# Two-way attention in exact-split products: the exponentials put in front of the next scaling, and energy's end in another order on VectorE, ScalarE and TensorE

## The chip, the cores and the metric

The kernel runs on one core of one Trainium2 chip. Its time is the device time of one execution in microseconds (us), the median of several runs. A profiled execution beside them gives the trace: every instruction of every engine with its start and its duration. The engines are PE (TensorE, matmuls), PEld (its weight loads), DVE (VectorE), ACT (ScalarE), POOL (GpSimd) and SP (SyncE, which issues DMAs). Each works through its own instructions in the order in which the program was written, and waits where a semaphore says so.

## What is computed

```python
x_q = jnp.einsum('oc,bcn->bno', w_qk, y)
x_k = jnp.einsum('oc,bcn->bon', w_qk, x)
x_v = jnp.einsum('oc,bcn->bon', w_v, x) + b_v[None, :, None]
energy = jnp.einsum('bnc,bcm->bnm', x_q, x_k)
attention = jax.nn.softmax(energy, axis=-1)
attention = attention / (1e-07 + attention.sum(axis=1, keepdims=True))
x_r = jnp.einsum('bcn,bnm->bcm', x_v, attention)
x_r = jax.nn.relu(jnp.einsum('oc,bcn->bon', w_t, x - x_r) + b_t[None, :, None])
return x + x_r
```

x and y (ctx_2048) are 32 x 256 x 1024 in fp32; there are 32 batches b, 256 channels and 1024 columns. The softmax goes along a row of the 1024 x 1024 energy, and the second normalisation along a column.

## The kernel before, in words

Everything stays on the one core, batch by batch (loop at L709). The weights are multiplied together ahead of the loop: energy is y' G x with G = w_qk' w_qk, and the values come with w_t already in them. PSUM's eight banks of 128 x 512 fp32 are one tile, `banks`.

**Energy** (class `Energy`, L420). A batch has NT = 8 tiles of 128 rows. A tile is 128 x 1024 and takes a pair of banks: pair n % 4, that is banks 2(n % 4) and the next, in all batches but the last, which has only three pairs (n % 3). y and G x are each held as three parts (`yf`, `gf`). `first` multiplies two of them, 8 matmuls, and lets ACT multiply the pair by a constant in place (`act.mul`, the "scaling"; for tile 7 each half for itself, right behind its own four matmuls). `second` adds the third part, 4 matmuls, and has DVE take the row's minimum (`nm`, a tensor_reduce over 1024). `exp` is ACT's exponential from the pair into `e`, with the minimum as bias; it sums the row (`rs`). `share` is DVE's reciprocal of that sum (`ri`) and the addition of the scaled row to `acc`, the column sums.

The order is written by hand (L713 to L765): each engine's instructions are issued in the order of the program (class `InOrder`). In iteration n stand first(n), second(n-1), exp(n-2) and share(n-3). On ACT the scaling of tile n so stands in front of the exponential of tile n-2. Below, first(n), scaled(n), second(n), nm(n), exp(n) and share(n) name these pieces of tile n.

**Seven products.** G x, the values and the last product are made by Strassen's scheme in Winograd's form (class `Seven`): seven products P1 to P7 in three banks. A method p1 to p7 is the matmuls of one product; p1, p5 and p6 are followed by ACT's copy out of the bank (`p1s`, `p5s`, `w`), and later products are added onto the same bank: P6, P7 and P4 onto P1's, P3 onto P5's. So P6 needs the copy p1s, P3 needs p5s, and P7 needs w. c11, c12, c22 are DVE's sums of a bank and a copy. For G x (class `Keys`, names with g: gp1s, gp5s, gw, result gfr) the banks are 0, 1, 2; for the values (class `Values`, names with u) 3, 4, 5. Banks 0 to 3 are those of tiles 4 and 5 (L748 on), banks 4 and 5 those of tile 6.

**Energy's end** (L740 to L765). While the last tiles are still at ACT and DVE, PE goes on with the next batch's G x and values. Then come the column sums (`columns`, a DVE instruction, output `parts`), their inverse `rc` on DVE, and the attention product (class `Attention`): DVE normalises the tiles of `e` (`normal`), forms their sums t1 to t4 (`mix`, tile `et`), and PE multiplies them. In the last batch nothing follows; the branch at L766 ends the batch before and then its own attention.

Of the kernel before, what the change touches and what calls it, by code (L numbers as in the profile page):

```python
# [17 lines left out]
def kernel(  # L18
# [26 lines left out]
    NT = N // P  # L45
    MB = 512
    MH = N // MB
# [8 lines left out]
    OVER = 1.0 + 2.0**-12  # L56
# [21 lines left out]
    pe, dve, act, pool = (InOrder(g) for g in (nc.tensor, nc.vector, nc.scalar, nc.gpsimd))  # L78
# [8 lines left out]
    def load(b, pieces=1):  # L87
        to = xp.tile([P, KC, N], F32, tag="x", name=f"x_{b}")
        from_ = x[b].rearrange("(k p) n -> p k n", p=P)
        W = KC // pieces  # L90
        for j in range(pieces):
            nc.sync.dma_start(to[:, ts(j, W)], from_[:, ts(j, W)])
        loaded[b] = to
# [115 lines left out]
    def temp(tag, name):  # L209
        return cp.tile([P, MB], F32, tag=tag, name=name)  # L210
# [8 lines left out]
    def summed(b):  # L219

        s = up.tile([P, 4, MB], F32, tag="xs", name=f"xs_{b}")
        t1, t3, t4, t2 = (s[:, j] for j in range(4))
        to = loaded[b]
        b11, b12 = to[:, 0, ts(0, MB)], to[:, 0, ts(1, MB)]
        b21, b22 = to[:, 1, ts(0, MB)], to[:, 1, ts(1, MB)]
        if b == 0:
            pool.tensor_tensor(t1, b11, b12, ALU.add)
            pool.tensor_tensor(t2, b22, t1, ALU.add)
            pool.tensor_tensor(t3, b12, b22, ALU.add)
            pool.tensor_tensor(t4, b21, t2, ALU.add)  # L230
            steps = []
        else:
            q = quarters(x[b])
            nc.sync.dma_start(s[:, :2], q[:, 0, 1:2, :].to_broadcast([P, 2, MB]))
            nc.sync.dma_start(s[:, 2:], q[:, 1])
            steps = [
                lambda: accumulate(s[:, :2], corners(x[b])),
                lambda: accumulate(s[:, 2:], s[:, 0:1].to_broadcast([P, 2, MB])),
                lambda: accumulate(t4, q[:, 1, 1]),
            ]  # L240
        return (b11, b21, b22, t4, t1, t2, t3), steps
# [178 lines left out]
    class Energy:  # L420
# [21 lines left out]

        def first(self):

            if self.n + 1 < NT:
                self.products((0, 1))
                act.mul(self.pair, self.pair, -OVER)
                return
            for h in range(MH):
                self.products((0, 1), (h,))  # L450
                act.mul(self.pair[:, h], self.pair[:, h], -OVER)

        def second(self):

# [177 lines left out]
    def columns(b):  # L632

        dve.tensor_reduce(
            parts[:, :, 0],
            acc.rearrange("p (j r) -> p j r", r=G32),
            AX.X,
            ALU.add,
            apply_transpose=True,
        )  # L640
# [5 lines left out]
    def inverse(b):  # L646


        sc = one.tile([P, NB, 1], F32, tag="sc", name=f"sc_{b}")
        s = sc[:, :, 0]  # L650
        for a in range(1, NG):
            moved(parts[:G32, :, a], parts[ts(a, G32), :, 0])
        dve.tensor_reduce(s[:G32], parts[:G32], AX.X, ALU.add)
        dve.reciprocal(s[:G32], s[:G32])
        moved(s[G32 : 2 * G32], s[:G32])
        moved(s[2 * G32 :], s[: 2 * G32])
        rc = one.tile([P, NB, G32], F32, tag="rc", name=f"rc_{b}")
        dve.transpose(rc.rearrange("p j r -> p (j r)"), sc.to_broadcast([P, NB, G32]))
        return rc.rearrange("p j r -> p (j r)")
# [8 lines left out]
    g = Keys(0, xr)  # L668
# [40 lines left out]
    for b in range(B):  # L709
        more = b + 1 < B  # L710
        rows = []

        for n in range(NT):  # L713
            now = Energy(b, n, q.to, g.split.to)
            rows.append(now)
            now.first()
            if n == 0:
                e = ep.tile([P, NT, N], F32, tag="e", name=f"e_{b}")
                acc = one.tile([P, N], F32, tag="acc", name=f"acc_{b}")
            if n > 0:  # L720
                rows[n - 1].second()
            if b == 0 and n == 1:
                u.p4()
                u.c21()
                xsteps[1]()
                xsteps[2]()
                ur, usteps = u.factors()
                for step in usteps:
                    step()
            if more and b > 0 and n == 0:  # L730
                load(b + 1)
                xn, xsteps = summed(b + 1)
            if n > 1:
                rows[n - 2].exp()
            if n > 2:
                rows[n - 3].share()
            if more and b > 0 and n in (2, 4, 6):
                xsteps[n // 2 - 1]()

        if more:  # L740
            q = Queries(b + 1)
            for i in range(KC):
                q.load(i, nc.sync.dma_start)
            g = Keys(b + 1, xn)
            rows[-1].second()
            rows[-2].exp()
            rows[-3].share()
            g.p1()  # L748
            rows[-1].exp()
            rows[-2].share()  # L750
            g.p5()
            g.p2()
            g.c11()
            rows[-1].share()
            g.p6()
            columns(b)
            g.p3()
            g.c12()
            g.p7()
            g.c22()  # L760
            un = Values(b + 1, xn)
            un.p1()
            un.p5()
            un.p2()
            un.p6()  # L765
        else:  # L766
            rows[-1].second()
            rows[-2].exp()
            rows[-3].share()
            before.xpart(before.one, 7, True)  # L770
            rows[-1].exp()
            rows[-2].share()
            before.epart(before.one, 7)
            ur, usteps = u.factors()
            now = Attention(b, xr, ur)
            now.begin()
            rows[-1].share()
            columns(b)
            for step in usteps:
                step()  # L780
            before.p7s = temp("w", "p7s")
            act.copy(before.p7s, before.one)
        rc = inverse(b)
        if more:
            q.parts(0)
            q.lower(0)
            un.p3()
            g.p4()
            g.c21()
            un.p7()  # L790
            q.parts(1)
            q.lower(1)
            q.mixed(0)
            g.split.parts(0)
            q.mixed(1)
            g.split.lower(0)

            def between():
                g.split.parts(1)
                g.split.lower(1)  # L800
                g.split.mixed(0)
                g.split.mixed(1)

            now = Attention(b, xr, ur)
            now.begin()
            now.run(un, between=between)
            pool.tensor_copy(behind, now.t4[:, HT - 1, :1])
            if b + 2 < B:
                now.close()
                ur, usteps = un.factors()  # L810
                for step in usteps:
                    step()
            else:
                now.epart(now.two, 3, (3,))
                now.c12()
                now.put()
            before = now
            xr, u = xn, un
        else:
            before.end()  # L820
            now.run(None, before)
            now.finish()
# [30 lines left out]
```

## Time and profile before

| | |
|---|---|
| time, median of 3 runs | 2147.12 us (2146.04 to 2147.6) |
| the profiled execution's own time | 2146.82 us |
| its span, first to last instruction | 2144.9 us |
| mean granted TensorE clock | 1.000 |
| busy: PE, DVE, ACT, POOL | 97%, 83%, 53%, 31% of the span |
| distance of two batches | 66.05 us (tile 6's minimum at 1040.06 and 1106.11) |

The page of the profile gives busy times, waits (an engine and a tile, the releaser, the us in total, how often, the longest) and groups of instructions by output and input. A row of a timeline is: start and duration in us, engine, line, operation, output<-input, shapes, how many were merged, and in brackets the idle time in front of it with its releaser. The line is L73 for nearly all, since a helper records every instruction; tiles tell them apart. Matmuls are pipelined: the recorded duration of one is longer than the distance to the next.

### The profile page before, as it was taken

Reading aid. Unit: us, or ns where it says so; the run is one execution under the profiler, and the core shown is the slowest. Engines: PE = TensorE matmul, PEld = TensorE weight load, DVE = VectorE, ACT = ScalarE, POOL = GpSimd, SP = SyncE. Lnnn points to the kernel's source line nnn. Section 1 sums busy time; section 2 is a strip of 40 time slices with the busy share of each in tenths; the row PEclk is TensorE's granted clock in tenths of the full one; section 3 lists DMA queues with packets and bytes.
Section 4 is the critical chain, followed back from the end, with each engine's and each line's share of the span. In section 5 each row is a group of like instructions: output and inputs, shape, how many; then the busy total and the mean of one; then the engine's idle time right before and its main releaser. Section 6 shows DMA issues by size and latency. Waiting matters only on the chain.

```text
span 2144.9 us, 21782 instructions
## 1 busy us (share of the span) xinstructions
PE 2085.0 (97%) x7586; PEld 1286.2 (60%) x7586; DVE 1778.6 (83%) x2264; ACT 1145.6 (53%) x1570; POOL 674.7 (31%) x574
## 2 busy tenths in 40 slices
PE   8999999999999999999999999999999999999988
PEld 6556666566665566555665656666556665566553
DVE  6898778897878887789887788888888788988877
ACT  5456545566454564545654556645456454565451
POOL 3331333313333223332233331333323333223321
PEclk9999999999999999999999999999999999999999
DMA  4766567665676655775657765567665577555740
GB/s 138 167 130 142 126 162 175 141 135 131 146 177 161 128 134 131 178 166 124 142 128 167 172 141 132 131 151 177 157 129 132 132 182 167 121 140 128 171 88 30
DMA packets 107788, 306.03 MB, mean 143 GB/s; under 512 B 10656, under 2 KB 11424, under 8 KB 107680
## 3 DMA queue, kind: packets, MB, share of 16 engines
q0 software_dynamic: 57040, 170.68, 43.4%
q1 hardware_dynamic: 50496, 133.85, 18.3%
q8 instruction: 60, 0.98, 0.2%
q14 instruction: 48, 0.39, 0.1%
q10 hardware_dynamic: 144, 0.13, 0.0%
HBM read 124.78 MB, written 33.55 MB: 74 GB/s over the span
## 4 chain that ended last, share of the span: by engine, by line
PE 88%; DVE 7%; ACT 3%; issue 1%; DMA 0%; SPq 0%; DVEq 0%; ACTq 0%
PE banks L73 88%; DVE nm L73 4%; DVE acc L73 2%; ACT e L73 2%; ACT gp5s L73 1%; DVE e L73 0%; DMA yfr<-in_ctx_dram 0%; ACT banks L73 0%; DVE et L73 0%; DVE ri L73 0%; ACT gf L73 0%; DVE parts L73 0%; DVE z L73 0%; DVE gfr L73 0%; DVE rc L73 0%
## 5 line engine op out<-in xcount | busy, mean ns | idle before, releaser
L73 PE MATMUL banks<-gf,yf 128*128 128x512 f32 x3072 | 716.9, 394 | 6.7 <-ACT e L73 6.7
L73 PEld LDWEIGHTS banks<-gf,yf 128*128 128x128 f32 x3072 | 576.3, 188 | 141.7 <-issue 14.8
L73 DVE TENSOR_REDUCE nm<-banks 128x1 f32<-128x1024 f32 x256 | 313.2, 1223 | 195.2 <-PE banks L73 184.0
L73 ACT ACTIVATE banks<-banks 128x1024 f32<-128x1024 f32 (+1 forms) x288 | 263.4, 915 | 190.2 <-PE banks L73 188.5
L73 PE MATMUL banks<-et,us 128*128 128x512 f32 x768 | 350.7, 597 | 0.8 <-DVE et L73 0.8
L73 DVE SCALAR_TENSOR_TENSOR e<-e,ri,rc 128x512 f32<-128x512 f32 x512 | 347.4, 745 | 1.1
L73 ACT ACTIVATE e<-banks,nm 128x1024 f32<-128x1024 f32 x256 | 284.7, 1112 | 45.1 <-DVE nm L73 45.1
L73 DVE SCALAR_TENSOR_TENSOR acc<-e,ri,acc 128x1024 f32<-128x1024 f32 x224 | 290.3, 1296 | 8.0
L73 PEld LDWEIGHTS banks<-et,us 128*128 128x128 f32 x768 | 143.2, 190 | 192.8 <-issue 161.7
L73 POOL DMA_DIRECT2D yf<-yfr x62 | 53.1, 856 | 567.0 <-ACT yf L73 567.0
L73 PE MATMUL banks<-e,ut 128*128 128x512 f32 x512 | 225.0, 592 | 3.1 <-DVE e L73 3.1
L73 ACT ACTIVATE z<-banks,bt 128x512 f32<-128x512 f32 x31 | 21.4, 689 | 342.6 <-DMA out_dram<-z 342.6
L73 PEld LDWEIGHTS banks<-e,ut 128*128 128x128 f32 x512 | 97.2, 190 | 125.9 <-issue 110.1
L73 DVE TENSOR_TENSOR et<-e 128x1024 f32<-128x1024 f32 x128 | 153.7, 1221 | 4.4
L73 POOL TENSOR_TENSOR ut<-ut,bu 128x1024 f32<-128x1024 f32 x64 | 156.7, 2575 | 0.0
L73 POOL DMA_DIRECT2D gf<-gf x62 | 53.1, 856 | 305.0 <-DMA gf<-gfr 260.7
L73 DVE SCALAR_TENSOR_TENSOR z<-z,x 128x512 f32<-128x512 f32 x96 | 138.3, 1441 | 3.3
L73 ACT ACTIVATE yf<-yf 128x1024 fp32r<-128x1024 f32 x124 | 124.3, 1050 | 2.0
L73 PE MATMUL banks<-e,us 128*128 128x512 f32 x256 | 125.3, 592 | 0.0
L73 ACT ACTIVATE gf<-gf 128x1024 fp32r<-128x1024 f32 x124 | 124.2, 1049 | 2.0
L73 PE MATMUL banks<-et,ut 128*128 128x512 f32 x256 | 115.1, 592 | 0.0
L73 POOL DMA_DIRECT2D xs<-xs x31 | 37.2, 1201 | 246.8 <-DMA xs<-in_x_dram 238.9
(104 smaller groups left out, 2600.4 us busy)
## 6 DMA issues: line engine op xcount, KB each, us to landing
yfr<-in_ctx_dram SPq DMA_DIRECT2D x64, 512.0 KB, 5.8
out_dram<-z SPq DMA_DIRECT2D x128, 256.0 KB, 3.4
x<-in_x_dram SPq DMA_DIRECT2D x31, 1024.0 KB, 7.4
xs<-in_x_dram SPq DMA_DIRECT2D x62, 512.0 KB, 5.0
yf<-yfr POOLq DMA_DIRECT2D x62, 512.0 KB, 5.2
yf<-yf POOLq DMA_DIRECT2D x62, 512.0 KB, 7.9
gf<-gfr POOLq DMA_DIRECT2D x62, 512.0 KB, 10.6
gf<-gf POOLq DMA_DIRECT2D x62, 512.0 KB, 5.2
```

The lines of the kernel that those rows point to most:

```text
L73: self.last = getattr(self.engine, name)(*args, **kwargs)
```

## The change

Three things are moved; no computation is added or taken away.

1. The scaling leaves `first` and becomes `scaled`; in iteration n exp(n-2) now stands in front of scaled(n). Tile 7's scaling is still done in two halves, but behind all eight of its first matmuls in the order of the program.
2. The shares go up by one tile inside the loop: share(n-2) in iteration n, from 2 to 6. At the end nm(6) and nm(7) follow each other on DVE, and the shares of tiles 5, 6 and 7 come behind them. c11, c12 and c22 of G x come behind the column sums.
3. G x's P5 with its copy p5s is issued in front of tile 7's exponential, and the values' P1 in front of G x's P7. On PE that is the only change of order: the values' P1 between P3 and P7.

```diff
         def first(self):
 
-            if self.n + 1 < NT:
-                self.products((0, 1))
-                act.mul(self.pair, self.pair, -OVER)
-                return
-            for h in range(MH):
-                self.products((0, 1), (h,))
-                act.mul(self.pair[:, h], self.pair[:, h], -OVER)
+            self.products((0, 1))
+
+        def scaled(self):
+
+            for at in (ts(0, MH),) if self.n + 1 < NT else (ts(0, 1), ts(1, 1)):
+                act.mul(self.pair[:, at], self.pair[:, at], -OVER)
...
             now.first()
-            if n == 0:
+            if n > 1:
+                rows[n - 2].exp()
+            now.scaled()
+            if n == 1:
                 e = ep.tile([P, NT, N], F32, tag="e", name=f"e_{b}")
                 acc = one.tile([P, N], F32, tag="acc", name=f"acc_{b}")
             if n > 0:
...
-            if n > 1:
-                rows[n - 2].exp()
-            if n > 2:
-                rows[n - 3].share()
+            if 1 < n < NT - 1:
+                rows[n - 2].share()
...
             rows[-2].exp()
             rows[-3].share()
             g.p1()
+            g.p5()
             rows[-1].exp()
             rows[-2].share()
-            g.p5()
+            rows[-1].share()
             g.p2()
-            g.c11()
-            rows[-1].share()
             g.p6()
             columns(b)
             g.p3()
-            g.c12()
-            g.p7()
-            g.c22()
             un = Values(b + 1, xn)
             un.p1()
+            g.p7()
+            g.c11()
+            g.c12()
             un.p5()
             un.p2()
             un.p6()
+            g.c22()
```

## The prediction

> **What bounds the kernel now.** I read the busy shares first, then the chain that ended last, then who waits for whom on PE.
>
> ```profile
> PE 2085.0 (97%) x7586; PEld 1286.2 (60%) x7586; DVE 1778.6 (83%) x2264; ACT 1145.6 (53%) x1570; POOL 674.7 (31%) x574
> PE 88%; DVE 7%; ACT 3%; issue 1%; DMA 0%; SPq 0%; DVEq 0%; ACTq 0%
> PE banks L73 <- ACT gp5s L73: 40.0, 31, 1.4
> PE banks L73 <- ACT e L73: 6.7, 5, 1.4
> PE banks L73 <- DVE e L73: 3.1, 1, 3.1
> ```
>
> PE is the bound, and only its holes can be won. Two thirds of them are one wait, once in each of the 31 batches that have a successor: PE waits for ScalarE's copy gp5s. Next I read one batch in order of time (start, duration, in us): PE, then ACT, then DVE.
>
> ```profile
> 1033.67 7.19 PE L73 MATMUL banks<-gf,yf 128*128 128x512 f32 x31
> 1040.70 1.02 PE L73 MATMUL banks<-x,g 128*128 128x512 f32 x2
> 1043.27 1.02 PE L73 MATMUL banks<-xs,gs 128*128 128x512 f32 x2
> 1045.58 1.13 PE L73 MATMUL banks<-x,gs 128*128 128x512 f32 x2 [1.28 <-ACT gp5s L73]
> ```
>
> ```profile
> 1037.35 1.11 ACT L73 ACTIVATE e<-banks,nm 128x1024 f32<-128x1024 f32 x1
> 1038.44 1.23 ACT L73 ACTIVATE banks<-banks 128x512 f32<-128x512 f32 x2
> 1039.58 1.11 ACT L73 ACTIVATE e<-banks,nm 128x1024 f32<-128x1024 f32 x1
> 1041.32 1.11 ACT L73 ACTIVATE e<-banks,nm 128x1024 f32<-128x1024 f32 x1 [0.54 <-DVE nm L73]
> 1043.85 1.11 ACT L73 ACTIVATE e<-banks,nm 128x1024 f32<-128x1024 f32 x1 [0.84 <-DVE nm L73]
> 1044.95 0.58 ACT L73 COPY gp5s<-banks 128x512 f32<-128x512 f32 x1
> ```
>
> ```profile
> 1037.34 1.23 DVE L73 TENSOR_REDUCE nm<-banks 128x1 f32<-128x1024 f32 x1
> 1040.06 1.23 DVE L73 TENSOR_REDUCE nm<-banks 128x1 f32<-128x1024 f32 x1
> 1041.39 1.28 DVE L73 SCALAR_TENSOR_TENSOR acc<-e,ri,acc 128x1024 f32<-128x1024 f32 x1
> 1042.60 1.22 DVE L73 TENSOR_REDUCE nm<-banks 128x1 f32<-128x1024 f32 x1
> ```
>
> (Times named below without a line are from these same timelines.) The reader sees a ladder: tile 7's minimum stands behind a share (1041.39) on DVE, tile 7's exponential behind that minimum, gp5s behind that exponential, and G x's P3 (1045.58) behind gp5s. P3 could have started at 1043.27 + 0.86 = 44.13 (products follow at 0.86: 1040.70, 41.56, 42.41, 43.27). So it loses 1.45, and the matmul pair then takes 1.13 instead of 1.02. **1.55 us a batch** can be won. The last batch has its own hole: it works with three pairs of banks, so a tile's first products wait for an exponential three tiles back.
>
> ```profile
> 2075.80 3.04 PE L73 MATMUL banks<-gf,yf 128*128 128x512 f32 x12 [1.30 <-ACT e L73]
> 2080.19 3.02 PE L73 MATMUL banks<-gf,yf 128*128 128x512 f32 x12 [1.35 <-ACT e L73]
> 2111.57 0.67 PE L73 MATMUL banks<-e,ut 128*128 128x512 f32 x1 [3.13 <-DVE e L73]
> ```
>
> Five such waits: 2080.19 - 2075.80 = 4.39 a tile where an undisturbed one takes 12 x 0.227 = 2.72 (31 matmuls in 7.19, the last lasting 0.39, give 0.227).
>
> **The change part by part.** No instruction is added or removed on any engine, and no DMA is moved past another; SP's and POOL's queues keep their order. Only the order on ACT, DVE and PE changes.
>
> *Exponential in front of scaling, tiles 2 to 6.* Count from the start t of the last matmul of tile n-2's second part. The minimum starts at t + 0.39 + 0.11 (second(6)'s last matmul starts at 39.57, nm at 40.06) and ends at t + 1.72. The exponential follows after 0.03, the next ACT instruction 1.09 after the exponential's start (37.35 to 38.44), so the scaling runs from t + 2.84 to t + 3.85. It used to start when its products were there, about t + 2.2. PE needs it for second(n), which stands behind first(n), second(n-1) and first(n+1): 20 matmuls, t + 21 x 0.227 = t + 4.76. Cover: 0.86 us. Cost nothing; if the minimum were over 0.86 late, each tile would cost the excess. DVE keeps PE's pace: reduce, reciprocal and share (37.34, 38.48, 38.67 to 39.96) take about 2.66 of a tile's 2.72 us now as then; the share is of a tile one later.
>
> *The same at tile 7: the price.* No first(8) stands between. Tile 5's minimum ends at 37.34 + 1.23 = 38.57, exp(5) starts at 38.60, the first half of the scaling at 39.69, ending at 40.29 (0.6 each half, 1.23 for two now). PE wakes 0.05 after its releaser (gp5s ended 45.53, P3 started 45.58): 40.34. Second(7) starts today at 40.86 - 0.39 - 3 x 0.227 = 39.79. It is held 0.55, and the next matmul after a hold is 0.11 late, as behind gp5s: its four matmuls end **0.66 later**. The second half is scaled by 40.78, in time for the third matmul (40.91). No row shows this wait. It can't be below nothing, since second(7) starts back to back today. The nearest rows bound it closer: 0.45 if the half scaling starts 0.1 earlier than I pair it, and 1.15 if PE had to have both halves (40.83 - 39.79, + 0.11). The longest hold behind an exponential in the trace, 1.67 (4.39 - 2.72), is the outer end. I take 0.66, since it is built from neighbouring rows.
>
> *P1, P5 and their copies in front of exp(7), and the shares behind nm(7).* P1 moves to 41.36 and the rest follows at 0.86: P5 42.22, P2 43.08, P6 43.93, P3 44.79, the values' P1 45.65, P7 46.54, the values' P5 47.43 (its eight small matmuls take 0.89). Who is late next? exp(6) waits for nm(6) as today, 41.32; gp1s at 42.43 to 43.00, P6 needs it at 43.93. gp5s when P5 has ended (43.24), to 43.85, P3 needs it at 44.79: the old wait is gone with 0.9 to spare. nm(7) is ready at 41.63 + 1.22 = 42.85, exp(7) follows gp5s at 43.8 to 44.9, gw follows P6's end to 45.6. P7 needs gw: behind P3 directly it would come at 45.65, on the edge; with the values' P1 between it comes at 46.54, 0.9 to spare. That is the cover this move gives. The values' P1 writes bank 3, free since exp(5). Today the values' P5 starts at 47.40 + 0.89 = 48.29, then at 47.43: PE wins **0.86 to 0.89**.
>
> *DVE.* After nm(7) three shares at 1.39 apart (45.31 - 43.92, the last three today) end at 47.03, the column sums (1.25) at 48.3, then c11, c12, c22 (0.68, 0.65, 0.67) at 50.1 against 51.03 now. So DVE is 0.95 earlier: one share less lies between nm(6) and the column sums, of whose 1.3 the wait for nm(7) eats 0.35. PE's products with t1 are held by DVE today by 0.06, so a batch can follow DVE: I take **0.92**. P4, which needs c22, keeps its distance.
>
> *Sum over 31 batches:* 31 x 0.92 = 28.5.
>
> *Last batch.* exp(n-3) now runs in front of scaled(n-1): done, with its accumulator read (1.2 in all), at t + 2.96, while first(n) can start at t + 13 x 0.227 = t + 2.95. Of 1.67 lost per wait at most 0.17 stays: 5 x 1.5 = 7.5 won. Tile 7's 0.66 is paid here too, so PE comes 6.9 earlier, but it then waits 3.13 for DVE's normalised tiles anyway. DVE: nm(6) 7.5 earlier, one share less before nm(7) (1.0 net), and one share less beside POOL's sums (2.34 and 2.10 against 1.28), about 0.8: 9.3. I take **9**, between 7 and 9.5.
>
> Total 37.5. The profiled execution took 2146.82 (span 2144.9); the median of the runs is 2147.12, 0.3 above. 2147.1 - 37.5 = **2109.5**. With 1.15 at tile 7: 31 x 0.43 + 8 = 21, 2125; with 0.45: 31 x 1.13 + 9.5 = 44.5, 2102.
>
> *A rule that speaks against it.* The row first: the reduce at 1037.34 takes 1.23, and the reciprocal behind it starts at 1038.48, 0.09 before its end; no DVE row here has a pause behind it. The Trainium skill, "VectorE: DVE Perf Modes", section "The DRAIN you can't avoid", says that a Vector instruction is followed by a drain of about its duration less 266 ns, save where the next is not held. By that (an estimate) each of the three shares lined up behind nm(7) would cost 1.0 more, the columns would come 3 later, and the gain of a batch would be lost. The trace decides; the sum has no such term.
>
> **The rivals.**
> 1. *The wait moves.* Second(7) is held for as long as P3 was, 1.55: if nm(5) came 0.9 later than today, since share(4) and nm(5) stand close on DVE. Then only the last batch gains: 2147 - 9 = 2138. Against it: nm(5) starts 0.11 behind PE's last matmul, as nm(6) does, so PE releases it, not DVE.
> 2. *DVE takes the gain back.* If the column sums or c22 came no earlier, t1 and all products behind it would stand where they stand now, and what PE wins in front is waited for later: between 0 and 0.4 a batch, 2125 to 2138. For it: PE is held 0.06 by t1 today. Against it: the 0.95 above.
> 3. *Slower: the scaling becomes late in every tile.* ACT is strictly in order, so a minimum that is late now delays the scaling behind it, and PE with it. It decides when the minimum comes over 0.86 late; 0.24 of wait in 5 tiles of 31 batches eats the whole 37.5, and 0.5 gives 78 - 37.5 = +40: 2187. For it: DVE has but 0.06 a tile to spare. Against it: nm starts at PE's pace 2.72 apart (37.34, 40.06), so nothing piles up.
> 4. *It doesn't do what it says:* gp5s still behind exp(7). In the built order gp5s stands in front, so this has next to no chance and counts with rival 1.
>
> **How the numbers follow.** Forecast (2102 to 2125) 0.80; rival 1 0.06; rival 2 0.05; rival 3 0.07; better than 2102 0.02. The range is the forecast's own, which leaves out 0.20. A measurement here can tell about 0.2% (4.3 us). Faster: 0.80 + 0.02 + rivals 1 and 2 but for 0.02 near their end = 0.91; same 0.02; slower 0.07.
>
> **What would show it.** The wait of PE for gp5s gone from PE's waits; a new one, second(7) on the scaling (ACT banks), 31 or 32 times at 0.4 of idle; the distance of two batches 65.1 instead of 66.06; the waits of the last batch near 0.1; the distance from nm(6) to the column sums, 8.56 now (48.62 - 40.06) and 7.0 then (47.06 - 40.06). I am wrong if PE waits for the scaling in tiles 2 to 6, if second(7)'s hold is over 1.2, or if PE waits for t1 by as much as it wins in front.

## The result and the profile after

The changed kernel takes **2109.45 us** (median of 4 runs, 2109.11 to 2110.49) against 2147.36 for the kernel before beside it: ratio 0.9823, 95% interval 0.9806 to 0.984. The profiled execution took 2109.47 (span 2107.7). The forecast was 2109.5, so the total is met to 0.1 us. That is closer than its terms were, as is shown below.

From the page of the changed kernel, busy time and the shares of the chain; then PE's waits, from the answer on who waits for whom:

```profile
PE 2083.9 (99%) x7586; PEld 1283.9 (61%) x7586; DVE 1778.4 (84%) x2264; ACT 1150.8 (55%) x1570; POOL 674.3 (32%) x574
PE 91%; DVE 3%; ACT 3%; issue 0%; DVEq 0%
```

```profile
PE banks L73 <- ACT banks L73: 13.4, 32, 0.9
PE banks L73 <- DVE gfr L73: 1.9, 1, 1.9
```

No engine has less to do: PE's busy time is the same to 0.1%, and only its share of a shorter span rose. The row for gp5s (40.0) is gone, those for ACT e (6.7) and DVE e (3.1) too. A new row has come, 32 times: PE waits for the scaling. The same place of a batch as before, from the timelines of PE, ACT and DVE (rows in between are left out):

```profile
1027.53 1.22 PE L73 MATMUL banks<-gf,yf 128*128 128x512 f32 x4 [0.39 <-ACT banks L73]
1028.58 1.02 PE L73 MATMUL banks<-x,g 128*128 128x512 f32 x2
1031.15 1.02 PE L73 MATMUL banks<-xs,gs 128*128 128x512 f32 x2
1032.01 1.02 PE L73 MATMUL banks<-x,gs 128*128 128x512 f32 x2
```

```profile
1025.78 1.12 ACT L73 ACTIVATE e<-banks,nm 128x1024 f32<-128x1024 f32 x1 [0.60 <-DVE nm L73]
1026.88 1.07 ACT L73 ACTIVATE banks<-banks 128x512 f32<-128x512 f32 x2
1028.50 1.11 ACT L73 ACTIVATE e<-banks,nm 128x1024 f32<-128x1024 f32 x1 [0.54 <-DVE nm L73]
1030.50 0.59 ACT L73 COPY gp5s<-banks 128x512 f32<-128x512 f32 x1 [0.27 <-PE banks L73]
1030.98 1.12 ACT L73 ACTIVATE e<-banks,nm 128x1024 f32<-128x1024 f32 x1
```

```profile
1027.24 1.23 DVE L73 TENSOR_REDUCE nm<-banks 128x1 f32<-128x1024 f32 x1
1028.85 1.23 DVE L73 TENSOR_REDUCE nm<-banks 128x1 f32<-128x1024 f32 x1 [0.39 <-PE banks L73]
1034.29 1.25 DVE L73 TRANSPOSE_TENSOR_REDUCE parts<-acc 128x32 f32<-128x1024 f32 x1
```

The reader sees P3 (1032.01) follow P6 at the usual 0.86, and second(7) (1027.53) held behind the scaling at 1026.88, which stands behind exp(5) at 1025.78. The column sums come 34.29 - 27.24 = 7.05 behind nm(6).

### The profile page after: what moved, and what is told of

Same layout as the page of the kernel before. It is cut to its first block, busy times and chain, and to the rows that moved or that the text cites. A ratio compares the mean times of both kernels' runs of the same rounds, so it can differ in the third digit from the quotient of the medians.

```text
span 2107.7 us, 21688 instructions
## 1 busy us (share of the span) xinstructions
PE 2083.9 (99%) x7586; PEld 1283.9 (61%) x7586; DVE 1778.4 (84%) x2264; ACT 1150.8 (55%) x1570; POOL 674.3 (32%) x574
## 4 chain that ended last, share of the span: by engine, by line
PE 91%; DVE 3%; ACT 3%; issue 0%; DVEq 0%
PE banks L73 91%; DVE nm L73 2%; ACT e L73 2%; ACT banks L73 1%; DVE e L73 1%; DVE et L73 0%; DVE acc L73 0%; DVE parts L73 0%; DVE rc L73 0%; DVE sc L73 0%; DVEq L73 0%; DVE z L73 0%; DVE ri L73 0%
## 5 line engine op out<-in xcount | busy, mean ns | idle before, releaser
L73 PE MATMUL banks<-gf,yf 128*128 128x512 f32 x3072 | 726.2, 395 | 13.5 <-ACT banks L73 13.4
L73 POOL DMA_DIRECT2D xs<-xs x31 | 37.2, 1201 | 261.1 <-DMA xs<-in_x_dram 251.6
L73 PEld LDWEIGHTS banks<-wvtTs,xs 128*128 128x128 f32 x768 | 98.2, 192 | 29.6 <-issue 29.6
```

What stands on the lines that cost most here:

```text
L73: self.last = getattr(self.engine, name)(*args, **kwargs)
```

## The experiments

Each ran with a profile and three rounds beside the kernel before on its chip. The numbers to compare are the ratios, since that kernel took 2149 to 2150 in these runs. "A batch" is the distance of two energy starts on PE in the steady part (the median there), 66.06 before and 65.13 after. Times "after energy's start" count from a batch's first energy matmul.

| kernel | median us | ratio (95%) | a batch |
|---|---|---|---|
| the change | 2109.45 | 0.9823 (0.9806 to 0.984) | 65.13 |
| e1, new end alone | 2148.77 | 0.9996 (0.9987 to 1.0005) | 66.06 |
| e2, exp in front alone | 2139.43 | 0.9951 (0.9937 to 0.9966) | 66.06 |
| e3, early shares alone | 2109.86 | 0.9813 (0.9797 to 0.983) | 64.93 |
| e4, change, tile 7 scaled first | 2094.71 | 0.9746 (0.9731 to 0.976) | 64.67 |
| e5, change, P7 first | 2110.2 | 0.9815 (0.9799 to 0.9832) | 65.14 |
| e6, change, tile 7 scaled whole | 2122.77 | 0.987 (0.9856 to 0.9885) | 65.54 |
| e7, change, copy behind exp(7) | 2109.83 | 0.9812 (0.9797 to 0.9826) | 65.13 |
| e8, e4 with the old end | 2103.05 | 0.978 (0.9766 to 0.9795) | 64.97 |
| e9, e4 less 0.6 of DVE | 2085.61 | 0.9704 (0.9689 to 0.9718) | 64.33 |
| e10, change less 0.6 of DVE | 2105.56 | 0.98 (0.9783 to 0.9816) | 65.04 |

### e1: the new end alone

```diff
             rows[-3].share()
             g.p1()
+            g.p5()
             rows[-1].exp()
             rows[-2].share()
-            g.p5()
+            rows[-1].share()
...
```

(the rest of energy's end as in the change; the loop as before.)

> The kernel before with the new energy's end alone: P5 and its copy in front of exp(7), the values' P1 in front of P7, c11, c12 and c22 behind the column sums. The loop stays as it was, so share(4) still stands between nm(6) and nm(7) on DVE. Theory (a batch follows DVE): PE's wait for gp5s goes, 1.55 us a batch, but the column sums stay at 8.0 to 8.6 us behind nm(6), so PE waits the same time later, for c22 and for t1: between 2144 and 2150, the same as before. Rival (PE's hole is all that counts): 31 x 1.55 = 48 less, 2099.

The same as before, as the theory had it. PE's waits, and the two places in a batch's timeline:

```profile
PE banks L73 <- DVE gfr L73: 21.1, 32, 1.9
PE banks L73 <- DVE et L73: 16.7, 31, 0.5
```

```profile
1044.43 1.02 PE L73 MATMUL banks<-x,gs 128*128 128x512 f32 x2
1051.39 1.12 PE L73 MATMUL banks<-xs,g 128*128 128x512 f32 x2 [0.62 <-DVE gfr L73]
1065.13 1.12 PE L73 MATMUL banks<-et,us 128*128 128x512 f32 x2 [0.54 <-DVE et L73]
```

P3 (1044.43) waits for nothing, so the wait that the prediction starts from is gone. But P4 (1051.39) waits for c22 and a product of t1 (1065.13) waits for DVE, and both together return all of it: from start to start PE loses 0.88 at P4 and 0.83 at t1, 1.71, where before it lost 1.55 for gp5s and 0.16 at t1. **Filling PE's hole is worth nothing here as long as DVE is no earlier.**

### e2: the exponential in front of the scaling, alone

(the scaling leaves `first` as in the change.)

```diff
             now.first()
+            if n > 1:
+                rows[n - 2].exp()
+            now.scaled()
...
-            if n > 1:
-                rows[n - 2].exp()
             if n > 2:
                 rows[n - 3].share()
```

> The kernel before with exp(n-2) in front of scaled(n) alone; shares and energy's end stay. Theory: second(7) is held 0.66 us, but that is spent inside the wait for gp5s, which stays at its place, because nm(7) still stands behind share(4): no change in 31 batches. The last batch loses its five waits, 7.5 to 9 us: 2138 to 2140. Rival (the hold adds to the wait): 31 x 0.66 - 8 = +12, 2159. Rival (the exponentials' place is what brings the gain): 2110.

2139.4. In the steady batches second(7) is held 0.56 and the matmul behind it another 0.11, and the loss in front of P3 is 0.74 instead of 1.45: the hold is spent inside the old wait. What is won comes from the last batch: its five waits, 1.46 to 1.53 each before, are at most 0.06 here.

### e3: the shares one tile earlier, alone

```diff
-            if n > 2:
-                rows[n - 3].share()
+            if 1 < n < NT - 1:
+                rows[n - 2].share()
```

> The kernel before with the shares one tile earlier in the loop, nothing else. Theory: nm(6) and nm(7) follow each other, 41.3 instead of 42.6; exp(7) starts at 42.9, the copy gp5s ends at 44.6, P3 at 44.64 instead of 45.58: PE gains 0.93 a batch, and DVE 1.28, so 29 in 31 batches, and some 2 in the last batch's end: 2114 to 2118, nearly as much as the whole change. Rival (ACT's order must change too): over 2135.

2109.9, better than I expected and as much as the whole change. PE's waits:

```profile
PE banks L73 <- ACT gp5s L73: 10.5, 31, 0.5
PE banks L73 <- ACT e L73: 6.7, 5, 1.4
```

The copy still stands behind exp(7), but exp(7) now starts at 24.37 after energy's start instead of 25.34, since nm(7) no longer stands behind a share. A quarter of the idle time is left (10.5 of 40.0). A batch takes 64.93: 1.13 less than before, where I had 0.93. The inverse's transpose on DVE stands at 32.9 after energy's start, against 34.37 before: DVE is 1.5 ahead and out of PE's way, and PE's small waits for t1 went with it (below, at e9). The last batch keeps its waits (6.7). That the totals of e3 and the change agree is chance: a batch is 0.20 shorter in e3, and its last batch is 7.4 longer (75.47 against 68.09). The exponentials' new place thus costs in the steady batches and pays in the last one.

### e4: tile 7's scaling in front of exp(5) again

```diff
-            if n > 1:
+            if 1 < n < NT - 1:
                 rows[n - 2].exp()
             now.scaled()
+            if n == NT - 1:
+                rows[n - 2].exp()
```

> The changed kernel, but at tile 7 the scaling stands in front of exp(5) as it did before. Theory: the hold of second(7), 0.67 a batch, goes; nm(7) is ready 0.35 earlier, and DVE, which then bounds a batch, is 1.28 ahead of the kernel before instead of 0.95. So 1.28 to 1.34 a batch is won over before, and 0.35 to 0.4 over the changed kernel: 2096 to 2099. Rival (exp(5) behind the scaling is late for bank 2 or 3, or PE alone sets the time): no better than 2109, or 31 x 0.67 = 21 better, 2088.

2094.7, **15 us better than the change** and the best of the versions that compute the reference. The hold is gone from PE's waits, and a batch takes 64.67, 0.46 less than with the change; I had expected 0.35 to 0.4, so the total lies below my range of 2096 to 2099. DVE's transpose stands at 33.0 after energy's start, 1.37 ahead of the kernel before, where I had 1.28.

### e5, e6, e7: three details of the change

```diff
# e5
-            un.p1()
             g.p7()
+            un.p1()
# e6
-            for at in (ts(0, MH),) if self.n + 1 < NT else (ts(0, 1), ts(1, 1)):
+            for at in (ts(0, MH),):
# e7
-            g.p5()
             rows[-1].exp()
+            g.p5()
```

> The changed kernel with G x's P7 in front of the values' P1 again. Theory: P7 would start 0.86 behind P3, at 27.18 after energy's start, and the copy gw that it waits for ends at 27.12; so the move of the values' P1 hides at most 0.1 a batch: 2109 to 2113. Rival (the move is a needed cover): 0.5 a batch, 2125.

> The changed kernel with tile 7 scaled in one instruction of 1024 instead of two of 512. Theory: second(7) must wait for all of it, 1.01 instead of 0.60, so the hold grows from 0.67 to 1.05; nm(7) and DVE come as much later: 32 x 0.38 = 12 more, 2120 to 2123. Rival (the hold has slack behind it, DVE bounds the batch anyway): 2110 to 2113.

> The changed kernel with G x's P5 and its copy behind tile 7's exponential again, as before the change. Theory: with the shares out of nm(7)'s way the exponential starts at 24.4 after energy's start, the copy ends at 26.1, and P3 needs it at 26.3: no change, 2109 to 2111. Rival (the copy's place is what took the wait away): the wait comes back, 0.5 to 1.5 a batch, 2125 to 2155.

All three as the theory had them. e5: PE stands 0.09 later behind P7, and that is absorbed by the wait for t1, so a batch stays at 65.14. e7: the copy starts at 25.52 instead of 24.81 after energy's start, and P3 still runs at 26.32: the copy's place does nothing in the changed kernel. There the hold at tile 7 brings P3 so late that a copy which ends at 26.11 is in time; without the hold P3 runs at 25.64 (e4), and such a copy is late (e8). e6: the hold is 0.98 instead of 0.56, with 0.11 behind it; a batch takes 0.41 more, 13 us in all. PE's wait for the scaling in e6:

```profile
PE banks L73 <- ACT banks L73: 26.7, 32, 1.2
```

### e8: e4 with the old energy's end

```diff
             g.p1()
-            g.p5()
             rows[-1].exp()
             rows[-2].share()
-            rows[-1].share()
+            g.p5()
             g.p2()
+            g.c11()
+            rows[-1].share()
...
```

(and so on to the end of the block: e1's edit taken back.)

> The kernel of e4 (tile 7 scaled in front of exp(5)) with the old energy's end: the early shares, and exp(n-2) in front of scaled(n) for tiles 2 to 6, alone. Theory: 31 batches gain as in e3 (66.06 to 64.93), and the last batch 8 to 9 beside: 2100 to 2103, so that the new end is worth 0.26 a batch once tile 7's hold is gone. Rival (the new end is worth nothing): 2095. Rival (without it the order loses most): over 2115.

2103.1, a batch 64.97. PE waits for the copy again, by as much as in e3:

```profile
PE banks L73 <- ACT gp5s L73: 10.7, 31, 0.5
```

That is a loss of 0.60 a batch, from start to start, of which 0.32 comes back at t1, where PE waits in e4 and not here. Without the hold, the new end is worth 0.3 a batch, 8 us; with the hold (the change) e7 and e5 show two of its moves worth nothing.

### e9 and e10: who bounds a batch

In e4 (e9) and in the change (e10), c11 of G x leaves DVE; ACT copies the bank, so the addition of p1s is left out of the computation.

```diff
-            g.c11()
             g.c12()
             un.p5()
+            act.copy(g.block(0, 0), g.three)
             un.p2()
```

> The kernel of e4 with c11 of G x taken from DVE: ACT copies the bank instead, behind the values' P5, so the sum with p1s is left out and the output is another one. That frees 0.6 us a batch on DVE in front of the column's inverse. Theory (in e4 DVE bounds the batch): PE's wait for t1, 0.34 a batch, goes, and PE bounds again: 31 x 0.34 = 10.5 less than e4, 2083 to 2087. Rival (PE bounds e4 already): 2094 as e4.

> The changed kernel with c11 of G x taken from DVE in the same way (ACT copies the bank, the sum with p1s is left out). Theory: in the changed kernel PE waits only 0.10 a batch for t1, since the hold of second(7) already makes PE late; so the same 0.6 of DVE is worth 31 x 0.10 = 3: 2105 to 2108. Rival (DVE alone bounds the changed kernel): 31 x 0.6 = 19 less, 2091.

The same 0.6 us of DVE is worth 0.34 a batch in e4 and 0.09 in the change. The row to read is that of the eight matmuls with t1: 3.60 long when they wait for nothing. In order: before, the change, e4, e9.

```profile
1063.06 3.76 PE L73 MATMUL banks<-et,us 128*128 128x512 f32 x8
```

```profile
1049.39 3.69 PE L73 MATMUL banks<-et,us 128*128 128x512 f32 x8
```

```profile
1041.54 3.92 PE L73 MATMUL banks<-et,us 128*128 128x512 f32 x8
```

```profile
1037.65 3.60 PE L73 MATMUL banks<-et,us 128*128 128x512 f32 x8
```

The waits are too short to show as idle time (in e4 0.06 of them does), since the recorded duration of a matmul (0.59) is longer than the distance to the next (0.43); they show in the length of the merged row. In the kernel before PE was held 0.16 here, with the change 0.09, in e4 0.32. So PE and DVE bound a batch together: in before, e1, the change, e4 and e6 the inverse's transpose stands 31.7 in front of the next energy (34.37, 34.37, 33.45, 33.0 and 33.85 of their batches), and in e3, e8 and e9, where the row is 3.60 or nearly so, it stands 31.96 to 32.03 in front.

## Why the prediction was right, point by point

**The wait for gp5s, 1.55 a batch:** gone, as worked out. But the prediction divided the credit wrongly. It had the moved copy and the moved P5 carry this. e3 shows that the shares alone take away 0.95 of the 1.55, and e7 that the moves add nothing, since the hold at tile 7 covers the rest. Only without that hold are they worth something (e8).

**The hold at tile 7, 0.66:** measured 0.56 + 0.11 = 0.67 in nearly all batches. e6 shows the mechanism: the hold grows with the length of the scaling in front (0.98 for one of 1024). e4 shows the price: without it 0.46 a batch.

**DVE 0.95 earlier, column sums at 7.0 behind nm(6):** the transpose 34.37 - 33.45 = 0.92, the sums at 7.05. e1 shows that this term was needed and not only PE's: it has PE's gain without it and takes 66.06.

**0.92 a batch:** 66.06 - 65.13 = 0.93. The hold by t1 that I took as 0.06 was 0.16, which is why e3 gave more than I expected of it: 0.95 in front of P3 and 0.16 here make 1.11 of its 1.13.

**The values' P1 as a cover for gw, "0.9 to spare":** the spare is there, but the cover hides only 0.09 (e5), and nothing in the total.

**Tiles 2 to 6 at no cost (cover 0.86):** no waits there in a steady batch. DVE also had more room than the prediction gave it: a minimum, a reciprocal and a share follow each other in 2.54 (nm(6) at 1040.06, nm(7) at 1042.60 before), not 2.66, so 0.18 of a tile's 2.72 is to spare and not 0.06. In the first batch the minimum does come late, as rival 3 asked: POOL's sums slow DVE's shares (2.24 instead of 1.28), the minima follow late, and the hold at tile 7 is 0.5 longer. From the timelines of DVE and PE of the changed kernel:

```profile
42.42 2.24 DVE L73 SCALAR_TENSOR_TENSOR acc<-e,ri,acc 128x1024 f32<-128x1024 f32 x1
```

```profile
50.10 1.21 PE L73 MATMUL banks<-gf,yf 128*128 128x512 f32 x4 [0.90 <-ACT banks L73]
```

So the first batch, from energy start to energy start, takes 0.37 more than before (67.05 against 66.68) and not 0.92 less. That isn't the order alone: in the profiled executions of e5 and e7, whose loop is the same, the hold of the first batch is 0.55 to 0.56 as in the others, and it takes 66.14 and 66.13.

**31 batches, 28.5:** up to the last batch's energy start 2066.64 - 2039.59 = 27.05. The first batch explains 1.29 of the difference of 1.45, and the work in front of it, 0.47 longer (26.77 against 26.30), the rest and a little more. That start lies between 25.9 and 29.2 in the twelve traces, with the same instructions up to there, so the 0.47 need not be an effect of the change. (The sum with a hold of 1.15 comes to 2125.8; the prediction has 2125.)

**The last batch, 9 (7 to 9.5):** 10.2 (78.26 before and 68.11 after, from its energy start to the span's end), over my bound. The five waits went as worked out. The term that failed is the shares beside POOL's sums: I let one of two become fast, 0.8, and both did, (2.34 - 1.28) + (2.10 - 1.28) = 1.88. The two shares before, with the POOL sum that the first of them meets:

```profile
2101.73 2.34 DVE L73 SCALAR_TENSOR_TENSOR acc<-e,ri,acc 128x1024 f32<-128x1024 f32 x1
2104.17 2.10 DVE L73 SCALAR_TENSOR_TENSOR acc<-e,ri,acc 128x1024 f32<-128x1024 f32 x1
```

```profile
2101.72 1.26 POOL L73 TENSOR_TENSOR us<-ut 128x512 f32<-128x512 f32 x1 [28.02 <-PE banks L73]
```

After the change the last share does meet POOL, but here POOL's sum is the one that is stretched, to 2.20. Nothing in the prediction foresaw this: the share starts 0.21 in front of the sum, and in e4, e8 and e9, where the sum starts 0.01 in front of the share, the share takes 2.34. DVE's timeline after the change, POOL's, and PE's where it had waited 3.13:

```profile
2064.67 1.28 DVE L73 SCALAR_TENSOR_TENSOR acc<-e,ri,acc 128x1024 f32<-128x1024 f32 x1
2066.07 1.28 DVE L73 SCALAR_TENSOR_TENSOR acc<-e,ri,acc 128x1024 f32<-128x1024 f32 x1
2067.46 1.28 DVE L73 SCALAR_TENSOR_TENSOR acc<-e,ri,acc 128x1024 f32<-128x1024 f32 x1
```

```profile
2067.67 2.20 POOL L73 TENSOR_TENSOR us<-ut 128x512 f32<-128x512 f32 x1 [21.04 <-PE banks L73]
2069.95 1.26 POOL L73 TENSOR_TENSOR us<-us,ut 128x512 f32<-128x512 f32 x1
```

```profile
2070.80 3.60 PE L73 MATMUL banks<-et,ut 128*128 128x512 f32 x8
2074.35 7.11 PE L73 MATMUL banks<-e,ut 128*128 128x512 f32 x16
```

27.05 + 10.15 = 37.2 against 28.5 + 9 = 37.5: a miss of -1.4 and one of +1.2 nearly cancel, which is luck (the first figures are the spans', 2144.9 - 2107.7). By the drain that the Trainium skill's "VectorE: DVE Perf Modes" describes ("The DRAIN you can't avoid"), which it puts behind every Vector instruction whose next one is held, the column sums would have come 3 us later (an estimate). In the changed kernel the three shares lined up behind nm(7) start 1.39 and 1.40 apart in the steady batch (1030.18, 1031.57, 1032.97), and the column sums, which read what the last share wrote, start 0.03 behind its end (1034.29), so no such drain is paid here.

**The rivals.** Rival 2 (DVE takes the gain back) is what e1 measures, and it happens in full where the shares stay. Rival 1, a hold as long as the old wait, came nowhere; rival 3 only in the first batch, as above.

What the runs don't settle: why a steady batch now and then takes some 0.35 more (before, two batches with 66.39 and 66.40; after, one with 65.49).

## What to carry to other kernels

When one engine waits, follow the wait to what stands in front of the releaser in its own queue, and ask whether the other engine of the pair gains as much; here the early shares gave DVE the time that made PE's gain last, and the new order around PE's wait gave nothing without them. When an instruction with a late input is put in front of another in an in-order queue, look at the last round of the loop by itself: the cover that holds in the body (0.86) is missing there, and an exception for that one round (e4) was worth 15 us of 2109. Waits shorter than the overlap of two matmuls don't appear as idle time; they are read from the length of a merged row.

## What the runs showed of the hardware that was not expected

Where a share of DVE and a sum of POOL run at the same time, the one that started second takes longer, and the one that started first is not lengthened by that meeting. It is so in all 45 such overlaps of the twelve traces. In the last batch before, the share at 2101.73 started 0.01 behind POOL's sum, which took 1.26, and the share took 2.34 instead of 1.28; the next sum (2103.06) started while that share ran and took 2.13, and the next share (2104.17) started while that sum ran and took 2.10. After the change the share at 2067.46 started first and stayed at 1.28, and POOL's sum took 2.20. What the second one loses is a little less than the overlap (1.06 of an overlap of 1.26). So a shift of some tenths of a us decides which engine pays, here by 1.9 us on the path.
